# Attention weights transposed in 32 x 32 blocks on VectorE and moved by plain transfers; scores of eight heads at a time

## The chip, the cores and the metric

The kernel runs on one core of a Trainium2 chip. Time is device microseconds of one execution. Before the change three runs took 1278.85, 1280.2 and 1283.92 us; the median is 1280.2. A profile is a record of one execution by the hardware; in it PE is the matrix engine (TensorE), PEld its weight loads, DVE the vector engine (VectorE), ACT the scalar engine (ScalarE), POOL is GpSimd, and SP is SyncE, which here does nothing but issue DMAs.

## The reference

A cross-attention and a feed-forward block with simulated 8-bit quantization, each with a residual; the change touches the attention alone.

```python
# x [32, 100, 256], ctx [32, 361, 256], mask [1, 1, 100, 361]; 16 heads of 64
Q = einsum("btd,hdk->bhtk", layernorm(x), WQ)
K = einsum("btd,hdk->bhtk", ctx, WK)
V = einsum("btd,hdv->bhtv", ctx, WV)
attn = softmax(Q @ K^T / sqrt(64) + mask * -1e9)        # [b, h, 100, 361]
x = x + concat_heads(attn @ V) @ WO
x = x + ffn(layernorm(x))    # two linear layers of quantized inputs and weights, exact gelu between
```

Everything is float32 in the attention.

## The kernel before

There are 32 batches of 100 queries (`T`) and 361 keys (`S`), and 16 heads in 8 pairs (`NHP`); a pair's 128 features fill the 128 partitions. Two pairs, or four heads, make a quarter `q` (`PAIRS` = 2, `NQ` = 4). Keys are cut into `NSC` = 3 chunks of 128. Batches come in groups of `G` = 4; `j` is a batch's place in its group.

For each batch the matrix engine makes `kT` (keys, `k_part`, line 282), `v` (values, `v_part`, line 313), the scores `sc` (`products`, line 437: 100 queries by 361 keys a head; two heads of a pair occupy the upper and the lower 64 rows of the array side by side) and `av` (weights times values, `attend`, line 542). Once in a group it makes the queries of the next group (`pq`, `q_part`, line 374, in the last batch of a group) and projects the finished group (`py`, `project_T`, line 579, in the first). Per-batch outputs of that projection are transposed back (`project_back`, `po`) and added to x in `residual`.

Softmax: VectorE adds the mask and takes the row's extreme (`minima`, line 451) from PSUM into one of eight buffers of `pb`; ScalarE takes exponentials in place (`exponentials`, line 465); VectorE divides by the sum (`divide`, lines 473 and 480). The product with `v` needs the weights with keys on the partitions, so they must be transposed. In whole batches this takes four steps: GpSimd copies the float32 weights of a pair into `apart`, low and high 16-bit halves separated (`send`, line 505); SyncE issues one transposing DMA per pair into `xT` (line 514); ScalarE joins the halves into `pT` (`join`, line 521); `attend` of the next batch reads `pT`. The first and the last batch are done in parts instead, and their weights are transposed on the matrix engine (`weights_T`).

Thirty batches are whole. For them `whole_batch` writes out the order of each engine's instructions by hand: engines run in program order. In each of its four quarters stand the scores and minima of four heads, their exponentials, and the `k_part` of two pairs of the next batch. After the second quarter comes `attend` for the batch before; in the third and the fourth the three `v_part` of one half of the heads. `rest` ends the batch with layer-norm statistics, residuals and the group's work. PSUM tiles come from one pool of eight banks, taken in turn, so a new tile waits until the one eight places back has been read. DMAs issued on SyncE rotate over eight completion semaphores; one waits until the DMA eight places back has landed.

The 8-bit weights of the feed-forward block are prepared in pieces spread over the batches (`quantize_weight`); their overall maximum is found by GpSimd.

Of the kernel before, what the change touches and what calls it, by code (L numbers as in the profile page):

```python
# [27 lines left out]
def kernel(  # L28
# [15 lines left out]
    nc = tc.nc  # L44
# [19 lines left out]

    TH, RH = T // 2, P // 2
    TP = RH + TH
    TR = -(-T // 16) * 16
# [96 lines left out]
    with ExitStack() as att:  # L164
# [16 lines left out]
        maskt = wpool.tile([T, S], F32, tag="maskt", name="maskt")  # L181
# [5 lines left out]
        pb = wpool.tile([TP, NB, SP], F32, tag="p", name="p")  # L187
        for t in cbuf:
# [4 lines left out]
            wpool.tile([P, PAIRS, G, TP], F32, tag=f"q{q}", name=f"q{q}") for q in range(NQ)  # L193
# [5 lines left out]
        for q in range(NQ):  # L199
            clear(q, 0)  # L200

        apart = [
            wpool.tile([TR, 2 * NSC * 2 * SC], I16, tag=f"apart{k}", name=f"apart{k}")
            for k in range(2)
        ]
        for t in apart:
            nc.gpsimd.memset(t[T // 32 * 32 :], 0.0)

# [34 lines left out]
        nc.scalar.dma_start(out=maskt, in_=mask)  # L243
# [62 lines left out]
        def v_part(b, h, s):  # L306

            c = cbuf[b % NCB]
            if s == 0:
                vs[b, h] = p1.tile([SC, NSC, E // 2], F32, tag=f"v{h}", name=f"v{b}_{h}")  # L310
            pv = bank(f"pv{b}_{h}_{s}")
            for dc in range(NDC):
                nc.tensor.matmul(  # L313
                    pv[:SC, :],
                    c[:, dc, s * SC : (s + 1) * SC],
                    wvt[h][:, dc, :],
                    start=(dc == 0),
                    stop=(dc == NDC - 1),
                )
            return nc.vector.tensor_copy(vs[b, h][:, s, :], pv[:SC, :])  # L320
# [46 lines left out]
        def q_part(g, q):  # L367
# [3 lines left out]
            for pair in range(PAIRS):  # L371
# [12 lines left out]
                for j in range(G):  # L384
# [9 lines left out]
                    qbuf[q][:, pair, j0:j1, :T],  # L394
                    pq[:, j0 * T : j1 * T].rearrange("p (j t) -> p j t", t=T),
# [3 lines left out]
        pTs, aTs = {}, {}  # L399

        def weights_T(i, pair, on_vector):
# [5 lines left out]
            for h in range(2):  # L407
# [8 lines left out]
            pT = pTs[i, pair] = p1.tile(  # L416
                [SC, 2 * NSC, T], F32, tag=f"pT{pair}", name=f"pT{i}_{pair}"
            )
# [9 lines left out]
        def products(i, pairs):  # L428
# [3 lines left out]
            n = TP if halved(b) else T  # L432
# [13 lines left out]
        def minima(i, pss):  # L446

            for h, ps in pss.items():
                n = ps.shape[0]
                ms[h] = small.tile([TP, 1], F32, tag=f"m{h}", name=f"m{i}_{h}", bufs=1)  # L450
# [6 lines left out]
        def exponentials(i, heads):  # L457
            if i not in sums:
                sums[i] = [
                    small.tile([TP, 2 * NHP], F32, tag=t, name=f"{t}{i}") for t in ("rsum", "r")  # L460
                ]
            n = TP if halved(steps[i][0]) else T
# [6 lines left out]
        def divide(i, heads, at_once=4, after=None):  # L469
            rsum, r = sums[i]  # L470
            n = TP if halved(steps[i][0]) else T
# [25 lines left out]
        xTs, NX = {}, 3  # L497

        def send(i, q):

            n = NSC * 2 * SC
            for pair in range(q * PAIRS, (q + 1) * PAIRS):
                src = apart[pair % 2]
                for k in range(2):
                    nc.gpsimd.tensor_copy(  # L505
                        src[:T, k * n : (k + 1) * n].rearrange("t (c l s) -> t c l s", c=NSC, l=2),
                        pb[:T, (2 * pair + k) % NB, :].bitcast(I16).rearrange(
                            "t (c s l) -> t c l s", c=NSC, l=2
                        ),
                    )  # L510
                xT = xTs[i, pair] = p1.tile(
                    [SC, 2 * NSC * 2, TR], I16, tag="xT", name=f"xT{i}_{pair}", bufs=NX
                )
                nc.sync.dma_start_transpose(out=xT, in_=src)

        def join(i, q):
            for pair in range(q * PAIRS, (q + 1) * PAIRS):
                pT = pTs[i, pair] = p1.tile(
                    [SC, 2 * NSC, T], F32, tag=f"pT{pair}", name=f"pT{i}_{pair}"
                )  # L520
                nc.scalar.copy(  # L521
                    pT.bitcast(I16).rearrange("s c (t l) -> s c t l", l=2),
                    xTs[i, pair][:, :, :T].rearrange("s (c l) t -> s c t l", l=2),
                )

        def attend(i, pairs=None):
# [5 lines left out]
            g, j = b // G, b % G  # L532
            if first == 0 and j == 0:
                aTs[g] = p1.tile([P, NHP, G, T], F32, tag="aT", name=f"aT{g}")
            for p0 in range(first, first + n, HP):
                m = min(HP, n)
                av = bank(f"av{i}_{p0}")
                for pair in range(p0, p0 + m):
                    for c in range(NSC):
                        for k in range(2):  # L540
# [4 lines left out]
                                pTs[i, pair][:, k * NSC + c, :],  # L545
# [102 lines left out]
        def quantize_weight(src, rows, dst, name, n, after):  # L648

            cols = rows * dst.shape[2] // NWP  # L650
            if n == 0:
                w = wpool.tile([P, rows, dst.shape[2]], F32, tag="wst", name=f"w{name}")
                load = nc.gpsimd.dma_start(out=w, in_=src.rearrange("(c p) f -> p c f", p=P))
                tc.add_manual_dep(load.ins, after.ins.name, SYNC)
                am = small.tile([P, NWP], F32, tag="am", name=f"am{name}")
                scales[name] = w.rearrange("p c f -> p (c f)"), am
                return
            wf, am = scales[name][:2]
            if n <= NWP:
                i = nc.vector.tensor_reduce(  # L660
                    am[:, n - 1 : n], wf[:, (n - 1) * cols : n * cols], AX.X, ALU.max,
                    apply_absolute_value=True,
                )
                tc.add_manual_dep(i.ins, after.ins.name, ORDER)
            if n == NWP:
                al = small.tile([P, NWP], F32, tag="aal", name=f"aal{name}")
                nc.gpsimd.partition_all_reduce(al, am, P, bass_isa.ReduceOp.max)
                scales[name] = wf, al
            if n == NWP + 1:
                sw = const.tile([P, 1], F32, tag=f"sw{name}", name=f"sw{name}")  # L670
                rw = small.tile([P, 1], F32, tag="rw", name=f"rw{name}")
                nc.vector.tensor_reduce(sw, am, AX.X, ALU.max)
                nc.vector.tensor_scalar(sw, sw, 1.0 / 127.0, 1e-8, ALU.mult, ALU.max)
                nc.vector.reciprocal(rw, sw)
                scales[name] = wf, sw, rw
            if n > NWP:
                p = slice((n - NWP - 1) * cols, (n - NWP) * cols)
                wi = small.tile([P, cols], I16, tag="wi", name=f"wi{name}_{n}")
                nc.scalar.activation(wi, wf[:, p], AF.Copy, bias=0.0, scale=scales[name][2])
                return lambda: nc.vector.tensor_scalar(  # L680
                    dst.rearrange("p c f -> p (c f)")[:, p], wi, 127.0, -127.0, ALU.min, ALU.max
                )

# [9 lines left out]
        nc.vector.tensor_scalar(maskt, maskt, 1e9, None, ALU.mult)  # L693
        warm(bank("warm0"), 7)
        k_start()
        for h in range(2):
# [4 lines left out]
        q_part(0, 0)  # L701

        todo = [
            n if n is None else (w, n)
            for w in ("1", "2") for n in (0, None, *range(1, 2 * NWP + 1))
        ]
        weights = {"1": (w1T, NDC, w1qt), "2": (w2T, NFC, w2qt)}

        def rest(i, ended, last, after=None):
# [3 lines left out]
            for h in ended:  # L715
# [3 lines left out]
                if k == 2 * (G - 2) + 1 and not whole(i):  # L719
                    ln1(g + 1, after)  # L720
                if g >= 1 and 2 <= k < 2 + G:
                    project_back(g - 1, k - 2)
                if k == 2 * (G - 2) + 1:
                    ln1_T(g + 1)
# [3 lines left out]
                if g >= 1 and k == 1:  # L728
# [3 lines left out]
        def part_of_batch(i):  # L732
# [6 lines left out]
            first_copied = None  # L739
            last = scores(i)  # L740
            if i >= 1:
                if whole(i - 1):
                    join(i - 1, NQ - 1)
                attend(i - 1)
            if b >= 1:
                for h in begun:
                    for c in range(NSC):
                        done = v_part(b, h, c)
                        if h == begun[0] and c == 0:
                            first_copied = done  # L750
# [7 lines left out]
            rest(i, ended, last, first_copied)  # L758
# [6 lines left out]
        def whole_batch(i):  # L765
# [5 lines left out]
            late = []  # L771
# [3 lines left out]
            for q in range(NQ):  # L775
                heads = range(2 * PAIRS * q, 2 * PAIRS * (q + 1))
                minima(i, products(i, range(q * PAIRS, (q + 1) * PAIRS)))
                if q == 1:
                    divide(i, range(2 * PAIRS))
                    send(i, 0)  # L780
                exponentials(i, heads)
                if q == 0 and b - 1 + NCB < B:
                    load_ctx(b - 1 + NCB)
                n = steps[i + 1][2] // NQ
                for pair in range(q * n, (q + 1) * n):
                    k_part(i + 1, pair)
                if q == 0 and whole(i - 1):
                    join(i - 1, NQ - 1)
                if q == 1:
                    attend(i - 1)  # L790
                    last = divide(i, heads)
                    send(i, 1)
                    for piece in todo[:2]:
                        if piece is not None:
                            w, p = piece
                            late.append(quantize_weight(*weights[w], w, p, last))
                    del todo[:2]
                if q >= 2:
                    join(i, q - 2)
                    for c in range(NSC):  # L800
                        v_part(b, q - 2, c)
                        if c == 0:
                            divide(i, heads)
                            send(i, q)
                if q == 2:
# [384 lines left out]
```

## Time and profile before

| what | value |
|---|---|
| median of three runs | 1280.2 us |
| the profiled execution's own time | 1282.56 us |
| its span in the profile | 1280.8 us |
| granted TensorE clock, mean | 0.993 |
| instructions | 21412 |
| packets moved by DMA | 355220, of which under 512 B 332094 |
| hardware queue of SyncE, share of the 16 DMA engines | 44.3% |
| DMA issues on SyncE for the weights | 240 (`xT<-apart`), 8 a batch |

How to read it: a page of the profile gives each engine's busy time and share of the span, the chain of work that ended last (followed back from the last instruction, at each step to what released it), and groups of instructions by source line with their count, busy time, mean duration, and the idle time before them with what ended it. The trace behind it also answers with a timeline of an engine (start, duration, what) and with a table of busy times by window. Instructions on one engine overlap at their ends, so the distance from start to start is what one costs in a row of them. A busy share of a matrix engine says that it always had an instruction in flight, not that each ran at its best.

### The profile page before, as it was taken

The numbers are of one execution on the slowest core, as the hardware profiler recorded it, in microseconds if no ns is written. First come the engines' busy times: TensorE is split into PE (matmuls) and PEld (weight loads), VectorE is DVE, ScalarE is ACT, GpSimd is POOL, SyncE is SP. The second block draws the span as 40 slices with busy tenths as digits, with TensorE's granted clock in tenths as the row PEclk, the third lists the DMA queues.
The fourth block names the chain that finished last, engine by engine and source line by source line (L and its number), as shares of the span: only waits on it lengthen the run. The fifth ranks groups of instructions, "written<-read, shape, count | busy, mean of one in ns | idle before, by whom it ended". The sixth has DMA issues, their size and how long they took to land.

```text
span 1280.8 us, 21412 instructions
## 1 busy us (share of the span) xinstructions
PE 1249.6 (98%) x7184; PEld 703.2 (55%) x7184; DVE 863.8 (67%) x2409; ACT 817.8 (64%) x1720; POOL 510.3 (40%) x674
## 2 busy tenths in 40 slices
PE   9999999989999999999999999999999999999858
PEld 4655555555555555555555555555555555556426
DVE  4577574776557765786657764787647774686897
ACT  2567566665476855674666755676657754764876
POOL 2044333462435532553435532554335533462250
PEclk9999999999999999999999999999999999999989
DMA  8165534474445543555445543555345534551113
GB/s 241 50 131 99 99 62 81 79 142 77 88 66 96 114 79 66 103 105 99 78 75 105 97 74 77 102 102 105 59 76 104 105 67 85 87 97 25 60 46 104
DMA packets 355220, 115.50 MB, mean 90 GB/s; under 512 B 332094, under 2 KB 353158, under 8 KB 355110
## 3 DMA queue, kind: packets, MB, share of 16 engines
q1 hardware_dynamic: 352032, 107.42, 44.3%
q0 software_dynamic: 2144, 5.38, 1.3%
q10 hardware_dynamic: 934, 1.34, 0.3%
q8 instruction: 56, 0.92, 0.3%
q14 instruction: 54, 0.44, 0.1%
HBM read 24.97 MB, written 6.55 MB: 25 GB/s over the span
## 4 chain that ended last, share of the span: by engine, by line
PE 89%; DVE 4%; ACT 3%; issue 2%; DMA 1%; POOL 1%; SPq 0%; DVEq 0%; ACTq 0%; POOLq 0%
PE pk L282 24%; PE pv L313 24%; PE sc L437 13%; PE av L542 11%; PE pq L374 7%; PE py L579 6%; ACT h L1032 2%; PE pf L1136 2%; DVE p L480 1%; DVE v L320 1%; PE po L563 1%; PE warm L161 1%; DMA wvt<-in_wv_dram 1%; ACT xqT L942 0%; PE pt L411 0%
## 5 line engine op out<-in xcount | busy, mean ns | idle before, releaser
L505 POOL COPY apart<-p 100x768 int16<-100x768 int16 x480 | 396.8, 860 | 609.0 <-DVE p L480 411.8
L465 ACT ACTIVATE p<-p,m 100x361 f32<-100x361 f32 (+1 forms) x512 | 299.1, 588 | 252.6 <-DVE m L451 252.0
L282 PE MATMUL pk<-c,wkt 128*128 128x361 f32 x1016 | 341.5, 479 | 0.3 <-ACT xnT L365 0.3
L313 PE MATMUL pv<-wvt,c 128*128 128x512 f32 x768 | 340.2, 592 | 1.0 <-DMA wvt<-in_wv_dram 1.0
L521 ACT COPY pT<-xT 128x1200 int16<-128x1200 int16 x240 | 309.8, 1336 | 34.9 <-DMA xT<-apart 34.9
L451 DVE CUSTOM_DVE_ANT_0 p<-sc,maskt 100x361 f32<-100x361 f32 x480 | 227.2, 529 | 131.1 <-PE sc L437 120.9
L480 DVE TENSOR_SCALAR p<-p,r 100x361 f32<-100x361 f32 (+1 forms) x512 | 266.5, 583 | 4.4
L282 PEld LDWEIGHTS pk<-c,wkt 128*128 128x128 f32 x1016 | 183.0, 189 | 152.4 <-issue 44.5
L313 PEld LDWEIGHTS pv<-wvt,c 128*128 128x128 f32 x768 | 145.7, 190 | 168.9 <-issue 147.3
L320 DVE COPY v<-pv 128x512 f32<-128x512 f32 x192 | 127.2, 682 | 137.7 <-PE pv L313 137.5
L437 PE MATMUL sc<-kT,q 64*100 64x361 f32 (+1 forms) x1024 | 191.4, 484 | 0.4
L542 PEld LDWEIGHTS av<-pT,v 128*64 128x64 f32 x3072 | 134.3, 138 | 22.0 <-issue 6.1
L542 PE MATMUL av<-pT,v 128*64 128x100 f32 x3072 | 141.5, 252 | 3.7 <-ACT kT L289 3.7
L437 PEld LDWEIGHTS sc<-kT,q 64*100 64x100 f32 (+1 forms) x1024 | 78.3, 163 | 91.9 <-issue 16.3
L289 ACT COPY kT<-pk 128x361 f32<-128x361 f32 x254 | 102.1, 448 | 27.9 <-PE pk L282 27.9
L465 ACT ACTIVATION_READ_ACCUMULATOR p<-p,m 100x1 f32 (+1 forms) x512 | 96.8, 189 | 0.0
L374 PE MATMUL pq<-xnT,wqt 128*128 128x400 f32 x256 | 87.9, 500 | 0.2 <-ACT xnT L365 0.2
L579 PE MATMUL py<-aT,wot 128*128 128x400 f32 x224 | 76.4, 499 | 0.0
L374 PEld LDWEIGHTS pq<-xnT,wqt 128*128 128x128 f32 x256 | 48.4, 190 | 38.8 <-issue 3.3
L579 PEld LDWEIGHTS py<-aT,wot 128*128 128x128 f32 x224 | 42.6, 190 | 34.0 <-issue 3.3
L586 ACT COPY yT<-py 128x400 f32<-128x400 f32 x14 | 6.9, 492 | 84.9 <-PE py L579 84.9
L473 DVE RECIPROCAL r<-rsum 100x4 f32<-100x4 f32 (+2 forms) x131 | 22.5, 172 | 56.4 <-ACT p L465 56.1
(142 smaller groups left out, 722.3 us busy)
## 6 DMA issues: line engine op xcount, KB each, us to landing
c<-in_ctxT_dram SPq DMA_DIRECT2D x31, 361.0 KB
xT<-apart SPq DMA_TRANSPOSE x240
x<-in_x_dram SPq DMA_DIRECT2D x8, 400.0 KB
xb<-xb POOLq DMA_DIRECT2D x32, 100.0 KB, 2.2
x<-xb SPq DMA_DIRECT2D x5, 384.0 KB
out_dram<-x SPq DMA_DIRECT2D x5, 256.0 KB
out_dram<-x SPq DMA_DIRECT2D x3, 384.0 KB
wqt<-in_wq_dram SPq DMA_DIRECT2D x4, 256.0 KB
```

The source lines that it names most:

```text
L282: nc.tensor.matmul(pk[:, :S], wkt[q][:, dc, col * P : (col + 1) * P], c[:, dc, :S], start=(dc == 0), stop=(dc == NDC - 1),)
L313: nc.tensor.matmul(pv[:SC, :], c[:, dc, s * SC : (s + 1) * SC], wvt[h][:, dc, :], start=(dc == 0), stop=(dc == NDC - 1),)
L320: return nc.vector.tensor_copy(vs[b, h][:, s, :], pv[:SC, :])
L374: nc.tensor.matmul(pq[:, :GT], wqt[q][:, dc, pair * P : (pair + 1) * P], xnTs[g][:, dc, :], start=(dc == 0), stop=(dc == NDC - 1),)
L437: nc.tensor.matmul(pss[h], qbuf[pair // PAIRS][k * DK : (k + 1) * DK, pair % PAIRS, b % G, :n], kT[k * DK : (k + 1) * DK, pair, :], start= ...
L451: done = nc.vector.tensor_tensor_reduce(pb[:n, h % NB, :S], ps, maskh if halved(steps[i][0]) else maskt, 1.0, BIG, ALU.add, ALU.min, ms[h] ...
L465: nc.scalar.activation(s, s, AF.Exp, bias=ms[h][:n], scale=-1.0, accum_out=sums[i][0][:n, h : h + 1])
L480: nc.vector.tensor_scalar(s, s, r[:n, h : h + 1], None, ALU.mult)
L505: nc.gpsimd.tensor_copy(src[:T, k * n : (k + 1) * n].rearrange("t (c l s) -> t c l s", c=NSC, l=2), pb[:T, (2 * pair + k) % NB, :].bitcast ...
L521: nc.scalar.copy(pT.bitcast(I16).rearrange("s c (t l) -> s c t l", l=2), xTs[i, pair][:, :, :T].rearrange("s (c l) t -> s c t l", l=2),)
L542: nc.tensor.matmul(av[k * DK : (k + 1) * DK, (pair - p0) * T : (pair - p0 + 1) * T], vs[b, pair // HP][:, c, h * DK : (h + 1) * DK], pTs[i ...
L579: nc.tensor.matmul(py[:, :GT], wot[:, c, dc * P : (dc + 1) * P], aT[:, c, :, :].rearrange("p j t -> p (j t)"), start=(c == 0), stop=(c == ...
```

## The change

1. **Transposition.** The copies into `apart`, the transposing DMAs and `join` are gone. Queries now lie in four blocks of 25 on partitions 0 to 24, 32 to 56, 64 to 88 and 96 to 120 (`QB` = 32, `NQB` = 4, `TB` = 25): `q_part` writes them so, with zeros between, the mask is loaded so, and scores have 128 stationary columns instead of 100. `blocks` transposes, on VectorE, one head's 128 x 384 weights within each block of 32 x 32, into an `xT` tile that holds four heads; there are two such tiles. `send` then carries the block of queries `k` and key block `m` from partitions 32k to 32m with a plain DMA on SyncE: 16 DMAs for four heads, each of 32 partitions x 3 chunks x 100 floats, 38.4 KB.
2. **pT** becomes two tiles of eight heads (`wide`), with a query block's 25 columns of a head in four runs, 200 floats apart; `attend` reads them in that form as the moving operand.
3. **Order.** `whole_batch` works in two halves of eight heads: eight scores, the minima, six exponentials, two `k_part`, two exponentials, two `k_part`, and then division, transposition and sending of two quarters. `attend` stands in the first half. The six `v_part` come after both halves in one run, those of the second half of the heads copied by ScalarE instead of VectorE. `rest` is split into `residuals` and `group_work`.
4. **Weights' maxima.** `weight_pieces` finds the overall maximum with two small transposes on the matrix engine and reductions on VectorE instead of GpSimd's reduction over partitions.

```diff
-        maskt = wpool.tile([T, S], F32, tag="maskt", name="maskt")
+        maskt = wpool.tile([P, S], F32, tag="maskt", name="maskt")
+        nc.gpsimd.memset(maskt, 0.0)
...
-        nc.scalar.dma_start(out=maskt, in_=mask)
+        for k in range(NQB):
+            nc.scalar.dma_start(
+                out=maskt[k * QB : k * QB + TB], in_=mask[k * TB : (k + 1) * TB]
+            )
...
-            return nc.vector.tensor_copy(vs[b, h][:, s, :], pv[:SC, :])
+            copy = nc.scalar.copy if h and not halved(b) else nc.vector.tensor_copy
+            return copy(vs[b, h][:, s, :], pv[:SC, :])
...
                 nc.vector.tensor_scalar(
-                    qbuf[q][:, pair, j0:j1, :T],
-                    pq[:, j0 * T : j1 * T].rearrange("p (j t) -> p j t", t=T),
+                    qbuf[q][:, pair, j0:j1, :].rearrange("p j (k t) -> p j k t", t=QB)[..., :TB],
+                    pq[:, j0 * T : j1 * T].rearrange("p (j k t) -> p j k t", k=NQB, t=TB),
                     -1.0 / DK**0.5, None, ALU.mult,
                 )
...
-        xTs, NX = {}, 3
+        xTs, NX, NH = {}, 2, 2 * PAIRS
+
+        def blocks(i, heads):
+            q = heads[0] // NH
+            xTs[i, q] = p1.tile(
+                [P, SP // QB, NH * TB + QB - TB], F32, tag="xT", name=f"xT{i}_{q}", bufs=NX
+            )
+            for h in heads:
+                nc.vector.transpose(
+                    xTs[i, q][:, :, h % NH * TB : h % NH * TB + QB],
+                    pb[:, h % NB, :].rearrange("t (c s) -> t c s", s=QB),
+                )
 
         def send(i, q):
-            n = NSC * 2 * SC
-            for pair in range(q * PAIRS, (q + 1) * PAIRS):
...
-                    nc.gpsimd.tensor_copy(
...
-                nc.sync.dma_start_transpose(out=xT, in_=src)
-
-        def join(i, q):
...
-                nc.scalar.copy(
...
+            src = xTs[i, q].rearrange("p (c m) t -> p c m t", c=NSC)
+            half, t0 = divmod(q * NH * TB, NHP * TB)
+            dst = wide(i, half).rearrange("s (c k) t -> s c k t", c=NSC)[..., t0 : t0 + NH * TB]
+            for m in range(P // QB):
+                for k in range(NQB):
+                    nc.sync.dma_start(
+                        out=dst[m * QB : (m + 1) * QB, :, k, :],
+                        in_=src[k * QB : (k + 1) * QB, :, m, : NH * TB],
+                    )
...
+            def weights(pair, k, c):
+                if not whole(i):
+                    return pTs[i, pair][:, k * NSC + c, :]
+                h = 2 * (pair % HP) + k
+                return wide(i, pair // HP)[:, c * NQB : (c + 1) * NQB, h * TB : (h + 1) * TB]
...
-                                pTs[i, pair][:, k * NSC + c, :],
+                                weights(pair, k, c),
...
-            for q in range(NQ):
-                heads = range(2 * PAIRS * q, 2 * PAIRS * (q + 1))
-                minima(i, products(i, range(q * PAIRS, (q + 1) * PAIRS)))
...
+            if b - 1 + NCB < B:
+                load_ctx(b - 1 + NCB)
+            for half in range(2):
+                heads = range(half * NHP, (half + 1) * NHP)
+                minima(i, products(i, range(half * HP, (half + 1) * HP)))
+                n = steps[i + 1][2] // 2
+                keys = range(half * n, (half + 1) * n)
+                exponentials(i, heads[:6])
+                for pair in keys[: n // 2]:
+                    k_part(i + 1, pair)
+                exponentials(i, heads[6:])
+                for pair in keys[n // 2 :]:
+                    k_part(i + 1, pair)
+                for q in range(half * NQ // 2, (half + 1) * NQ // 2):
+                    divide(i, range(2 * PAIRS * q, 2 * PAIRS * (q + 1)))
+                    blocks(i, range(2 * PAIRS * q, 2 * PAIRS * (q + 1)))
+                    send(i, q)
+                if half == 0:
+                    attend(i - 1)
+            residuals(i, range(2), None)
+            if j == G - 2:
+                ln1_T(g + 1)
+            v_part(b, 0, 0)
...
+            for c in range(1, NSC):
+                v_part(b, 0, c)
+            while later:
+                normalize(later.pop(), None)
+            for c in range(NSC):
+                v_part(b, 1, c)
+            if j == G - 3:
+                ln1(g + 1)
+            group_work(i, range(2))
```

## The prediction

> **What bounds the kernel now.** I read the busy shares and the chain of waits first.
>
> ```profile
> PE 1249.6 (98%) x7184; PEld 703.2 (55%) x7184; DVE 863.8 (67%) x2409; ACT 817.8 (64%) x1720; POOL 510.3 (40%) x674
> PE 89%; DVE 4%; ACT 3%; issue 2%; DMA 1%; POOL 1%; SPq 0%; DVEq 0%; ACTq 0%; POOLq 0%
> ```
>
> TensorE is busy 98% and is 89% of the chain. Shares average over stages, so the table by window comes next, from one `av` stage to the next: two plain batches, and two that also hold `py` or `pq`.
>
> ```profile
> 687.75:719.51 31.76, 31.76 (x198) 18.07 (x200) 25.80 (x74) 22.96 (x52) 15.59 (x21) 1.00 0.57 100
> 719.51:760.89 41.38, 41.38 (x218) 22.91 (x220) 25.80 (x71) 26.72 (x56) 15.99 (x21) 1.00 0.45 84
> 655.91:687.75 31.84, 31.78 (x191) 17.48 (x192) 23.50 (x73) 22.07 (x50) 18.41 (x26) 1.00 0.58 102
> ```
>
> TensorE fills every batch: 31.8 us in a plain one, 41.4 in a long one. So the POOL copies, the DMA transposes and the `join` copies, long as they are, stand beside TensorE; removing them buys nothing by itself. A gain must come out of TensorE's own rows:
>
> ```profile
> 611.83 2.69 PE L282 MATMUL pk<-c,wkt 128*128 128x361 f32 x8
> 614.46 4.34 PE L542 MATMUL av<-pT,v 128*64 128x100 f32 x96
> 618.73 1.46 PE L437 MATMUL sc<-kT,q 64*100 64x361 f32 x8
> 620.12 2.69 PE L282 MATMUL pk<-c,wkt 128*128 128x361 f32 x8
> 622.65 5.31 PE L313 MATMUL pv<-wvt,c 128*128 128x512 f32 x12
> 627.89 1.46 PE L437 MATMUL sc<-kT,q 64*100 64x361 f32 x8
> ```
>
> From start to start, `pk` takes 2.63 us before `av` and 2.53 before `pv`: a change of stationary shape costs time. Single starts show a score group of four heads as 0.384, 0.303, 0.308 and 0.397 us per pair of heads, of which 0.30 is streaming; the `pk` behind it begins with 0.408 instead of 0.303.
>
> **TensorE's part of the change.** Eight heads together: 0.384 + 6 x 0.305 + 0.397 = 2.61 us against 2 x 1.39, so 0.35 saved a batch. `pk` in runs of 16: 5.05 against 5.25 and 4.96 against 5.06, 0.30 saved. `pv` in one run: 0.09. Stationary 128 columns instead of 100: loads run inside the 0.30 us slots, except one per group, whose exposed part was 0.083 us at 100 columns (first start to load-bound second) and 0.106 at 128 (`pk`): 2 x 0.024 back. Net **0.7 us a batch**. The four one-row transposes for the weights' scale are under 1 us in all.
>
> `av` now streams 100 columns as four runs of 25, 800 B apart. No row has a strided moving operand. Below nothing is excluded, since the columns are the same. The nearest row is `av` itself (43.6 ns an instruction); at an assumed tenth more it would cost 0.43 us a batch, 13 in all. The Trainium skill (SBUF — State Buffer, Door 1: The DMA port swizzle) says that a 16-byte line read at least twice in a row goes at full rate; runs of 25 floats meet that but for at most one line each. I take nothing.
>
> **What leaves.** Per batch 16 POOL copies, 8 transposing DMAs and 8 `join` copies:
>
> ```profile
> L505 POOL COPY apart<-p 100x768 int16<-100x768 int16 x480 | 396.8, 860 | 609.0 <-DVE p L480 411.8
> L521 ACT COPY pT<-xT 128x1200 int16<-128x1200 int16 x240 | 309.8, 1336 | 34.9 <-DMA xT<-apart 34.9
> ```
>
> VectorE's divisions then run undisturbed; four took either of these:
>
> ```profile
> 654.85 2.49 DVE L480 TENSOR_SCALAR p<-p,r 100x361 f32<-100x361 f32 x4
> 658.95 1.36 DVE L480 TENSOR_SCALAR p<-p,r 100x361 f32<-100x361 f32 x4
> ```
>
> Start to start 0.32 us each when POOL is quiet, about 0.9 beside a POOL copy.
>
> **What VectorE gets.** 16 transposes of 384 columns. Not in the trace; the nearest row, the minima (361 columns), repeats every 0.455 us, which scales to **0.48**; bounds 0.4 and double, 0.9. A plain batch: 16 x 0.455 minima, 16 x 0.32 divisions, 0.8 reciprocals, 16 x 0.48 transposes, 1.8 for three `v` copies (the other three go to ScalarE, which loses 310 us), two residuals with statistics 3.5, normalizing 0.7, some 1.6 for semaphore waits ahead of the transposes (an estimate from the 21 ns records): 28.5 of 31.1 us. It fits, without much room. ScalarE isn't late: with 0.58 us an exponential, heads 0 to 3 are ready 2.9 us after the first minimum, when VectorE is still at its eight minima (3.7), and heads 6 and 7, behind two `kT` copies of 0.35, after 6.0, before the first division and its transposes end (7.1). Eight score tiles fill all eight PSUM banks, so the `pk` behind them waits for the first minimum, done 1.5 us after the scores begin and needed at 2.61: free, unless VectorE comes late to it.
>
> **What only moves.** The context load stands at the head of the batch, ahead of the first send on SyncE, 0.5 us counted below. The residuals, `ln1_T` and `ln1` change places within the batch with the same instructions; VectorE does the residuals before the `v` copies, counted below. The weights' maxima leave POOL (two reductions of 0.4 us) for VectorE and TensorE; their 1 MB loads stay on POOL. Three more mask loads of some 0.45 us stand on ScalarE's queue before its first copy at 10.1 us; the first scores come after 23 us, so that is hidden; without that cover it would cost 1.4 us once.
>
> **What SyncE gets: the step that decides.** 4 sends of 16 transfers, 64 a batch instead of 8, each 32 partitions x 3 x 400 B = 38.4 KB. The packets are light: 256 B packets took 18 ns and 1024 B ones 46, so 400 B is about 23, six per engine, 0.15 us. The queue's own timeline shows what an issue costs:
>
> ```profile
> 12.85 0.37 SPq L222 DMA_DIRECT2D wqt<-in_wq_dram  x1
> 13.27 0.47 SPq L222 DMA_DIRECT2D wkt<-in_wk_dram  x1
> 13.78 0.47 SPq L222 DMA_DIRECT2D wqt<-in_wq_dram  x1
> 14.29 0.98 SPq L215 DMA_DIRECT2D c<-in_ctxT_dram  x2
> 15.32 0.47 SPq L250 DMA_DIRECT2D wot<-in_wo_dram  x1
> 15.83 14.69 SPq L228 DMA_DIRECT2D x<-in_x_dram  x7
> ```
>
> Back to back, each with one satisfied wait, as in `send`, the pitch is **0.512 us** (13.27, 13.78, 14.29, 15.32 after two, 15.83). Without a wait, at the start, it was 0.46; alone, 0.37 plus a 0.045 gap, 0.42. I take 0.51, the row nearest in kind. The Trainium skill (DMA: Bandwidth & Descriptors, Issuing engines are not separate DMA queues) calls the sequencer's issue time usually small relative to the DMA itself. By it SyncE hides and the sum is TensorE's alone, 30 x 0.7 = 21 us gained. By the row 64 x 0.512 + 0.3 for the extra waits + 0.5 for the context load = **33.6 us a batch**, above the 31.1 that TensorE wants in a plain one. The row decides.
>
> What queues behind it: let A be the start of `av` for the previous batch. The first send waits until that `av` has read the first half of `pT`, A + 2.45. There are two `xT` tiles, so the transposes of the fourth quarter wait for the second send: A + 2.45 + 32 x 0.512 + 0.15 + 1.0 for landing (the last output DMA began at 1277.67 us, took 0.35 to issue, and its last packet ended at 1279.23, 1.2 later with eight 1 KB rows per engine; here there are six short ones) = A + 20. Behind them on VectorE: 2.3 of transposes and waits, residuals 3.5, `v` 1.8, normalizing 0.7, the next batch's first minimum 0.55, which frees the bank of the next `pk`, then 5.05 of `pk`: the next `av` at A + 33.9. So both the queue and this chain give 33.6 to 33.9; a plain batch grows from 31.8 to **33.7**. Long batches, 41.4, swallow it and lose 0.7.
>
> **Sum.** The chain has about 15 plain and 15 long intervals: 15 x 1.9 = +28; 15 x 0.7 = -10.5. At 270 us the present kernel once waits 4.78 us for `xT` with a slower `av` after it (5.79 instead of 4.27), 6 us in all; half of that may vanish, -3. Together +14.5: the profiled execution's 1282.6 (span 1280.8 and 1.8 around it) becomes 1297; it lay 2.4 above the median 1280.2, so I forecast **1295**.
>
> **Rivals.**
> 1. *SyncE keeps up, faster.* Decided by the pitch alone. At 0.46 the VectorE chain is A + 32.2: 15 x 0.4 - 13.5 gives 1273; at 0.42 nothing waits: -24, 1256. For it: the pitches without a wait, and that TensorE does lose work. Against: each transfer carries a wait. It is faster below 0.46 and slower above 0.49. Chance 0.24.
> 2. *The two cancel,* pitch 0.46 to 0.49, 1274 to 1286. Chance 0.14.
> 3. *VectorE becomes the bound:* transposes at 0.9 us add 6.4 to 28.5, and waits on `xT` on top: 35.4 a plain batch, 15 x 3.6 - 13.5, 1321. Nothing in the trace speaks for half rate, but nothing shows the operation. Chance 0.14.
> 4. *TensorE cools:* idle gaps of 2 us each may cost clock; after the 3.7 us gap at 270 the granted clock was 0.90 in that stretch. 15 x 1.5 on top of the forecast, 1317. Chance 0.08.
>
> The forecast itself has 0.40, with its own range 1284 to 1308. What a measurement can tell from no change is 0.5%, 6.4 us: faster below 1273.8, slower above 1286.6. From the cases: faster 0.24, same 0.14, slower 0.62. The range goes from 1256 (pitch 0.42) to 1330 (case 3 with some of case 4).
>
> **What would show it.** TensorE: score groups 2.6 us, `pk` runs 5.0, `av` still 4.27 when not waiting; long intervals 40.7. SyncE: 16 issues of a send in 8.2 us and no rest in plain batches. VectorE: a gap before the fourth quarter's transposes, released by a DMA; divisions 0.32 apart; transposes 0.48. Plain intervals near 33.7. I am wrong if SyncE idles in plain batches (issue under 0.46), if plain intervals fall to 31, or if transposes need 0.9.

## The result, and the profile after

The changed kernel takes **1508.1 us** (median of 4 runs, 1506.6 to 1509.6) against 1280.7 before (4 runs, 1278.9 to 1283.9): ratio 1.177, 95% interval 1.1745 to 1.180. The forecast was 1295, slower, with a range up to 1330. The sign and the place were right; the size was not.

The page of the changed kernel, its span, its busy shares and its chain of waits:

```profile
span 1505.7 us, 22604 instructions
PE 1349.9 (90%) x7186; PEld 774.8 (51%) x7188; DVE 959.9 (64%) x2803; ACT 584.9 (39%) x1570; POOL 111.9 (7%) x195
SPq 39%; PE 36%; DVE 7%; issue 6%; DMA 5%; POOL 5%; ACT 1%; DVEq 0%; ACTq 0%; POOLq 0%
```

Before, TensorE was 89% of the chain and SyncE's queue 0%. Now the largest share, 39%, is SyncE's issuing. The timeline of SyncE in the middle of the program (start us, duration us, what, count):

```profile
898.15 43.23 SPq L533 DMA_DIRECT2D pT<-xT  x64
941.48 0.53 SPq L215 DMA_DIRECT2D c<-in_ctxT_dram  x1
942.12 42.55 SPq L533 DMA_DIRECT2D pT<-xT  x64
984.78 0.53 SPq L215 DMA_DIRECT2D c<-in_ctxT_dram  x1
```

Sixty-four issues took 43.23 us, 0.675 each, and the next batch began 0.64 us after the context load did. There is no rest: 43.97 us from one batch to the next, where the forecast had 33.6. Nor does SyncE stand for its eight semaphores: a transfer lands 1.9 us after its issue begins (median), and eight issues take over 5 us. The same batches on TensorE, and its waits:

```profile
887.72 5.12 PE L285 MATMUL pk<-c,wkt 128*128 128x361 f32 x16
892.77 3.31 PE L561 MATMUL av<-pT,v 128*64 128x100 f32 x72
898.81 1.26 PE L561 MATMUL av<-pT,v 128*64 128x100 f32 x24 [2.73 <-DMA pT<-xT]
900.00 2.70 PE L451 MATMUL sc<-kT,q 64*128 64x361 f32 x16
902.63 5.12 PE L285 MATMUL pk<-c,wkt 128*128 128x361 f32 x16
907.59 10.46 PE L316 MATMUL pv<-wvt,c 128*128 128x512 f32 x24
```

The last quarter of `av`, 24 instructions, stands 2.73 us for its transfers. VectorE waits at the other end of the same queue; these are the lines with the largest such waits (total us, times, longest):

```profile
DVE xT L521 <- DMA pT<-xT: 369.4, 81, 7.8
PE av L561 <- DMA pT<-xT: 53.0, 21, 7.5
```

From the third start of `av` (67.6 us before, 66.9 now) to that of the last whole batch (1153.8 and 1370.2) there are 30 intervals, 14 of them long, with `py` or `pq` in them, and 16 plain. They summed to 1086.2 us before and to **1303.3** now, 43.4 each, which is SyncE's time for a batch. Long and plain ones no longer differ: they have means of 43.6 and 43.3 us now, and had 41.5 and 31.6 before. The sum grew by 217.1; the stretch after them is 8.6 longer and the one before 0.7 shorter, in all the 225 us by which the span grew. TensorE, which now rests, shows a granted clock of 0.921 over the span against 0.993.

### The profile page after: what moved, and what is told of

Same layout as the page of the kernel before. It is cut to its first block, busy times and chain, and to the rows that moved or that the text cites. A ratio compares the mean times of both kernels' runs of the same rounds, so it can differ in the third digit from the quotient of the medians.

```text
span 1505.7 us, 22604 instructions
## 1 busy us (share of the span) xinstructions
PE 1349.9 (90%) x7186; PEld 774.8 (51%) x7188; DVE 959.9 (64%) x2803; ACT 584.9 (39%) x1570; POOL 111.9 (7%) x195
## 4 chain that ended last, share of the span: by engine, by line
SPq 39%; PE 36%; DVE 7%; issue 6%; DMA 5%; POOL 5%; ACT 1%; DVEq 0%; ACTq 0%; POOLq 0%
SPq L533 39%; PE pk L285 9%; PE pv L316 9%; PE pq L378 5%; DMA pT<-xT 4%; PE sc L451 4%; PE py L598 4%; PE av L561 3%; DVE xT L521 2%; PE pf L1164 1%; POOL xb L143 1%; DVE p L465 1%; POOL rstd L646 1%; ACT h L1060 1%; DVE x L150 1%
## 5 line engine op out<-in xcount | busy, mean ns | idle before, releaser
L521 DVE STREAM_TRANSPOSE xT<-p 128x384 f32<-128x384 f32 x480 | 277.7, 579 | 399.0 <-DMA pT<-xT 369.4
L479 ACT ACTIVATE p<-p,m 128x361 f32<-128x361 f32 (+1 forms) x512 | 299.1, 587 | 304.8 <-DVE m L465 304.8
L451 PE MATMUL sc<-kT,q 64*128 64x361 f32 (+1 forms) x1024 | 253.4, 557 | 54.1 <-DVE rmax L622 46.2
L465 DVE CUSTOM_DVE_ANT_0 p<-sc,maskt 128x361 f32<-128x361 f32 x480 | 222.9, 529 | 42.7 <-PE sc L451 42.4
L451 PEld LDWEIGHTS sc<-kT,q 64*128 64x128 f32 (+1 forms) x1024 | 121.4, 214 | 165.6 <-DVE rmax L622 64.8
L494 DVE TENSOR_SCALAR p<-p,r 128x361 f32<-128x361 f32 (+1 forms) x512 | 174.3, 404 | 4.4
L324 ACT COPY v<-pv 128x512 f32<-128x512 f32 x90 | 52.8, 586 | 256.4 <-PE pv L316 256.4
L568 ACT COPY aT<-av 128x400 f32<-128x400 f32 (+2 forms) x67 | 31.9, 476 | 175.8 <-PE av L561 175.8
L479 ACT ACTIVATION_READ_ACCUMULATOR p<-p,m 128x1 f32 (+1 forms) x512 | 96.1, 188 | 0.0
L324 DVE COPY v<-pv 128x512 f32<-128x512 f32 x102 | 65.0, 676 | 12.5 <-PE pv L316 12.4
```

Source lines behind the costliest of these rows:

```text
L324: return copy(vs[b, h][:, s, :], pv[:SC, :])
L451: nc.tensor.matmul(pss[h], qbuf[pair // PAIRS][k * DK : (k + 1) * DK, pair % PAIRS, b % G, :n], kT[k * DK : (k + 1) * DK, pair, :], start= ...
L465: done = nc.vector.tensor_tensor_reduce(pb[:n, h % NB, :S], ps, maskh if halved(steps[i][0]) else maskt, 1.0, BIG, ALU.add, ALU.min, ms[h] ...
L479: nc.scalar.activation(s, s, AF.Exp, bias=ms[h][:n], scale=-1.0, accum_out=sums[i][0][:n, h : h + 1])
L494: nc.vector.tensor_scalar(s, s, r[:n, h : h + 1], None, ALU.mult)
L521: nc.vector.transpose(xTs[i, q][:, :, h % NH * TB : h % NH * TB + QB], pb[:, h % NB, :].rearrange("t (c s) -> t c s", s=QB),)
```

## The experiments

The question was why an issue costs 0.66 and not 0.51, and whether that is all. The rivals: the number of issues (**Theory 1**), the two `xT` tiles, which tie VectorE to the queue (**Theory 2**), and the bytes and packets behind the issues (**Theory 3**). Each kernel ran once where no number of runs is given. The pitch is the time from the start of one issue to the start of the next.

**The issue by itself (issue).** A bench in which nothing of the layer is computed: sixteen DMAs of one form after another from SyncE, for six forms between SBUF and SBUF (four are shown), one of them again from ScalarE, four weight loads and the output stores.

```diff
+    for n in range(N):      # da: the form of the change
+        nc.sync.dma_start(out=da[:32, n], in_=s4[32:64, :, 1, :100])
+    for n in range(N):      # db: 32 x 100
+        nc.sync.dma_start(out=db[32:64, n], in_=s4[:32, 0, 1, :100])
+    for n in range(N):      # dc: 32 x 3 x 200
+        nc.sync.dma_start(out=dc[64:96, n], in_=s4[32:64, :, 1, :200])
+    for n in range(N):      # dd: 128 x 3 x 100
+        nc.sync.dma_start(out=dd[:, n], in_=s4[:, :, 1, 100:200])
```

> Nothing of the attention or the feed-forward block is computed; the kernel only issues DMAs back to back on SyncE, 16 of each form, and writes zeros as output. In the changed kernel one issue of 32 partitions x 3 x 100 floats took 0.597 us and the next began 0.642 after it. If the pattern's dimensions set the cost: form a (32 x 3 x 100) 0.64 us again, c (32 x 3 x 200) and d (128 x 3 x 100) the same, b (32 x 100) and e (128 x 100) about 0.46 to 0.51, f (32 x 2 x 100) like a. If the number of rows sets it: d, with four times the rows of a, well over 0.7, and b well below e. If the bytes set it: c longer than a. If it is peculiar to the large kernel: a about 0.51 here.

SyncE's timeline of the bench:

```profile
4.01 12.73 SPq L65 DMA_DIRECT2D da<-src  x16
16.79 10.09 SPq L68 DMA_DIRECT2D db<-src  x16
26.92 10.27 SPq L71 DMA_DIRECT2D dc<-src  x16
37.23 10.79 SPq L74 DMA_DIRECT2D dd<-src  x16
```

Divide the last three by 16: 0.63 to 0.67 us an issue. The first form, that of the change, has a median pitch of 0.655; one gap of 2.7 us makes its row longer. ScalarE issued the same form at the same time, every 0.657 us: two queues side by side hardly slowed each other. Against the 0.641 that the form of the change has alone (next run), a third of the bytes (`db`), twice the bytes (`dc`) and four times the rows (`dd`) cost the same within 5%, so that neither dimensions nor rows nor bytes set the pitch, and it isn't peculiar to the large kernel. The two weight loads from DRAM that follow each other in this bench were 0.517 apart, near the row that the forecast had used. So the row was read rightly, but it wasn't a row of this operation.

**Which ends (ends).** The form of the change with its ends in SBUF or DRAM, and on fewer partitions; nothing of the layer is computed.

```diff
+    for n in range(N):      # sa: SBUF to SBUF
+        nc.sync.dma_start(out=sa[:32, n], in_=here)
+    for n in range(N):      # db: SBUF to DRAM
+        nc.sync.dma_start(out=rb[:32, n], in_=here)
+    for n in range(N):      # sc: DRAM to SBUF
+        nc.sync.dma_start(out=sc[:32, n], in_=away)
+    for n in range(N):      # de: DRAM to DRAM
+        nc.sync.dma_start(out=re[:32, n], in_=away)
```

> Nothing of the layer is computed: only DMA issues from SyncE, 16 of each kind, back to back. The form of the change (32 partitions x 3 x 400 B) with its ends in SBUF or DRAM. Theory A (an issue costs by its ends: two in SBUF are the dearest): SBUF to SBUF 0.64 us again, SBUF to DRAM near 0.41, DRAM to SBUF near 0.51, at the same 38.4 KB. Theory B (an issue costs by its form, 32 rows of three 400 B pieces): all four kinds at about 0.64. The same form SBUF to SBUF on 16, 8 and 4 partitions: if the cost goes with the engines or rows that take part, it falls below 0.6 with 8 or 4; if it is the instruction's own, it stays at 0.64.

```profile
4.47 10.26 SPq L73 DMA_DIRECT2D sa<-src  x16
14.77 7.67 SPq L76 DMA_DIRECT2D db<-src  x16
22.48 7.38 SPq L79 DMA_DIRECT2D sc<-away  x16
29.91 10.04 SPq L82 DMA_DIRECT2D de<-away  x16
50.82 11.69 SPq L87 DMA_DIRECT2D sh<-src  x16
```

The same 38.4 KB cost 0.641 us from SBUF to SBUF, 0.472 to DRAM, 0.464 from DRAM, and 0.633 from DRAM to DRAM (medians). Theory B falls. Theory A had the direction of the two mixed kinds (forecast 0.41 and 0.51), but the last kind shows that what is dear is not SBUF at both ends but **both ends in the same memory**. The packets don't explain it: they were of 400 B where the source was in SBUF and of 1200 B where it was in DRAM, and with either source it was the destination in the other memory that was cheaper. Why, these runs don't show. On 8 partitions (`sh`) it was 0.729, on 4 it was 0.690: fewer rows don't make it cheaper.

**A third of the data (third).** All 64 transfers, each with one chunk of its three; the other two chunks of the weights are zeros.

```diff
-                        out=dst[m * QB : (m + 1) * QB, :, k, :],
-                        in_=src[k * QB : (k + 1) * QB, :, m, : NH * TB],
+                        out=dst[m * QB : (m + 1) * QB, 0, k, :],
+                        in_=src[k * QB : (k + 1) * QB, 0, m, : NH * TB],
```

> The changed kernel with only the first of three key chunks carried by each of the 64 transfers of a batch (32 partitions x 100, two dimensions); the other chunks of pT are set to zero by GpSimd, so attention sees a third of the weights. Theory 1, SyncE's issue is the limit: the time follows the pitch of this form; at 0.50 us 64 x 0.50 + 0.9 = 33 us a plain batch, some 1290 us; at 0.64 no change from 1508. Theory 3, the transfers' bytes or packets are the limit: a third of them, so well below 1300 even if the pitch stays at 0.64.

```profile
888.64 41.94 SPq L534 DMA_DIRECT2D pT<-xT  x64
```

1490.7 us, pitch 0.633 (median). Two thirds of the transfers' packets gone bought 17 us of 227: bytes and packets are not the limit, and Theory 3 falls.

**Four tiles (nx4).** `NX` = 4 instead of 2; to make room, the feed-forward weights' preparation is left out.

```diff
-        xTs, NX, NH = {}, 2, 2 * PAIRS
+        xTs, NX, NH = {}, 4, 2 * PAIRS
```

> The changed kernel with four xT tiles instead of two; to make room, the preparation of the 8-bit feed-forward weights is left out (they are constants). Theory 1, SyncE's issue is the limit: 64 issues of 0.66 us stay, VectorE's 369 us of waiting shrink or move, and the time stays at 1490 to 1508. Theory 2, VectorE's wait for one of two xT tiles holds up the minima and so the scores: the time falls to 1250 to 1320.

```profile
PE av L561 <- DMA pT<-xT: 172.9, 32, 9.3
```

1499.4 us: VectorE's 369 us of waiting for the queue are gone, `av` waits 173 us for its transfers instead of 53, and the time stays. Theory 2 falls as the cause of the loss.

**Half the issues (eight, then eightfull).** Eight heads in a tile, so that a transfer is 32 partitions x 3 x 800 B and a batch needs 32. In `eight` the feed-forward weights' preparation is left out; in `eightfull` it is there, with the weights loaded in 1 KB pieces, twice, so that the wider tiles fit.

```diff
-        xTs, NX, NH = {}, 2, 2 * PAIRS
+        xTs, NX, NH = {}, 2, NHP
...
-                    send(i, q)
+                send(i, half)
```

> The changed kernel with eight heads in an xT tile and one send per half: 32 transfers a batch of 32 partitions x 3 x 200, the same bytes; the preparation of the 8-bit feed-forward weights is left out. Theory 1: SyncE needs 32 x 0.66 + 0.8 = 22 us a batch and hides, TensorE is the limit again: plain intervals 31.1, long 40.7, 1245 to 1262 us. Theory 3, bytes: no change, about 1500. Theory 2 would also allow about 1255, since each tile then has half a batch more time; nx4 tells it apart.

> The changed kernel with eight heads in a tile instead of four: 32 transfers of 32 partitions x 3 x 800 B a batch, and the feed-forward weights loaded twice in 1 KB pieces so that the wider tiles fit. Theory 1 (SyncE's issues are the whole loss): 32 x 0.655 + 0.8 = 21.8 us a batch hides beside TensorE; plain intervals 31.1, long ones 40.7, 1258 to 1268 us, faster than before by 1 to 1.7%. Rival (the lighter weights' preparation of the earlier eight-head kernel was part of its 1262): 1275 or more.

1262.0 us for `eight` (one run), and for `eightfull` **1260.0** (4 runs, 1259.4 to 1262.3) against 1280.8: ratio 0.983, interval 0.981 to 0.985. The rival of `eightfull` falls with it: the weights' preparation costs nothing that shows here. SyncE and TensorE in `eightfull`:

```profile
891.19 22.17 SPq L534 DMA_DIRECT2D pT<-xT  x32
913.46 0.53 SPq L215 DMA_DIRECT2D c<-in_ctxT_dram  x1
931.88 22.30 SPq L534 DMA_DIRECT2D pT<-xT  x32
```

```profile
908.76 10.91 PE L599 MATMUL py<-aT,wot 128*128 128x400 f32 x32
919.60 2.71 PE L451 MATMUL sc<-kT,q 64*128 64x361 f32 x16
922.23 5.12 PE L285 MATMUL pk<-c,wkt 128*128 128x361 f32 x16
927.28 4.35 PE L562 MATMUL av<-pT,v 128*64 128x100 f32 x96
931.56 2.70 PE L451 MATMUL sc<-kT,q 64*128 64x361 f32 x16
```

Thirty-two issues take 22.2 us; in this long batch SyncE then rests 18 us, and TensorE goes from stage to stage without a wait. Plain intervals are 31.1 to 31.4 us, but for three shorter ones at the ends, long ones 40.7 to 41.0.

The Trainium skill (Perfetto Trace Analysis, What "DMA-bound" means) names this kind of bound: the issuing engine's track solid with DMA slices. It has large descriptors (the pieces into which a DMA is cut) as the remedy. The trace agrees with the first. To the second it adds that the size of the pieces does nothing by itself: those of 800 B (`dc`) were issued no faster than those of 400 B (`sa`), 0.641 against 0.641. What helped was half as many transfers, each twice as large.

**Another queue (poolhalf).** The other way out, every second transfer from GpSimd's queue:

```diff
-                    nc.sync.dma_start(
+                    (nc.gpsimd if m % 2 else nc.sync).dma_start(
```

> The changed kernel with every second transfer issued by GpSimd's queue: 32 a batch on SyncE, 32 on GpSimd. Theory 1 (the loss is the issuing queue, not the 64 transfers): SyncE 32 x 0.655 + 0.8 = 21.8 us a batch, GpSimd, nearly idle otherwise, at up to 0.9 us each 29 us; both under 31.1, so 1256 to 1275 us. Rival (64 transfers a batch are too many for whatever moves them, or GpSimd's issue costs 1 us and more): 32 us and more a batch, 1290 us and above.

1334.5 us, the rival's side, but not by either of its reasons: GpSimd's issue had a median pitch of only 0.537 us, and SyncE rests again. GpSimd's timeline in a plain batch:

```profile
885.90 4.95 POOL L533 DMA_DIRECT2D pT<-xT  x9 [2.05 <-PE ptx L366]
891.12 3.78 POOL L533 DMA_DIRECT2D pT<-xT  x7 [0.27 <-DMA pT<-xT]
894.92 0.26 POOL L645 TENSOR_SCALAR v<-mv 100x1 f32<-100x1 f32 x1
```

The residual's step at 894.92 had its input when VectorE's statistics of the first residual ended, at 890.90, and stood behind 7 issues. VectorE's normalizing then waits for GpSimd:

```profile
899.14 0.73 DVE L150 TENSOR_SCALAR x<-x,mv,rstd 100x256 f32<-100x256 f32 x2 [4.83 <-POOL xb L143]
```

Behind it `pk` stood 1.67 us for VectorE's first minimum. Over the whole program (total us, times, longest):

```profile
DVE x L150 <- POOL xb L143: 61.4, 13, 7.1
PE pk L285 <- DVE m L465: 54.1, 15, 8.6
```

The first was 14.0 us in the changed kernel. The second was 6.2 us in `eightfull`, and those 48 us more are most of the 74.5 us between the two remedies. Moving an issue delays what is queued behind it on the other engine.

**Is the pitch all? (fifty, fifty4).** With 50 of the 64 transfers SyncE's batch costs some 34 us, about what the forecast had thought for 64. The blocks left out of the weights are zeros, written by GpSimd. `fifty4` adds four `xT` tiles, with the weights in 1 KB pieces as in `eightfull`.

```diff
+                nc.gpsimd.memset(wides[b, half][96:, :, :], 0.0)
...
+                    if m == 3 and k >= 1 - q % 2:
+                        continue
```

> The changed kernel with 50 of the 64 transfers of a batch; the blocks left out are zeros, so that part of the weights is missing from the sums. If only the pitch of the forecast's sum was wrong, 50 x 0.655 + 0.3 + 0.5 = 33.6 us of SyncE a batch, which is what the forecast had for 64, and its other terms then hold: plain intervals near 33.7, long ones near 40.7, some 1295 us (1285 to 1305). If something else of the change costs as well (two tiles, the slower transposes, a cooler TensorE), plain intervals stay above 36 and the time above 1320.

> The kernel with 50 transfers a batch (blocks left out are zeros), now with four xT tiles instead of two and the feed-forward weights loaded in 1 KB pieces to make room. In the run with two tiles SyncE needed 34 us a batch, but plain intervals took 37 to 39: VectorE's fourth transposes waited 4 us for a tile, and the residuals, GpSimd's steps, the normalizing and the next minimum queued behind them. Theory V (that chain behind the xT tiles holds the plain batch once SyncE is lighter): with four tiles the transposes don't wait, plain intervals fall to 34 to 35 (SyncE's 33.2 plus the landing), long ones stay 40.7, some 1300 to 1330 us. Rival (SyncE's load itself, or TensorE cooled by idling, holds it): plain intervals stay at 36.5 or more, 1370 or more.

1397.7 and 1347.3 us. In both the first `av` comes late, at 54.4 and 55.4 us against 31.7. The clearing changed GpSimd's order at the start: the first group's `rstd` stands behind it and behind a broadcast, at 36.0 us in `fifty` instead of 15.5. That is an artefact of the experiment, and without it they would be near 1375 and 1324, an estimate. The 30 intervals are free of it: 1178.4 (39.3 each) and 1121.9 (37.4), where the forecast's 33.7 and 40.7 have a mean of 37.2.

So in `fifty` 12 of the 14 long intervals are at 40.7 or 40.8, as forecast, but the plain ones have a mean of 37.3, in the middle in pairs of 39 to 41 and 35 to 38. The first of such a pair, from its `av` at 881.83 (A), VectorE, then TensorE:

```profile
902.45 2.42 DVE L522 STREAM_TRANSPOSE xT<-p 128x384 f32<-128x384 f32 x4 [4.23 <-DMA pT<-xT]
...
908.46 1.88 DVE L324 COPY v<-pv 128x512 f32<-128x512 f32 x3
912.08 0.73 DVE L150 TENSOR_SCALAR x<-x,mv,rstd 100x256 f32<-100x256 f32 x2 [1.75 <-POOL xb L143]
912.73 1.38 DVE L350 TENSOR_SCALAR xn<-x,mv,rstd 100x256 f32<-100x256 f32 x4
914.03 0.53 DVE L466 CUSTOM_DVE_ANT_0 p<-sc,maskt 128x361 f32<-128x361 f32 x1
```

```profile
914.62 6.66 PE L285 MATMUL pk<-c,wkt 128*128 128x361 f32 x16 [3.16 <-DVE m L466]
```

The fourth transposes start at A + 20.6 (A + 20 in the forecast). Then the forecast's chain lacks 1.75 us for GpSimd's step of the residual, which VectorE's normalizing needs, and 1.3 us for the next group's `xn`, which only the first of each pair holds. And `pk`, after 3.16 us of idle, takes 6.6 us instead of 5.05: its row in the table by window has a granted clock of 0.76 (column after the busy times), the next `pk` 1.00. The trace's record of the clock has half speed from 910.93 to 917.76 us and full speed on either side.

```profile
914.62:921.21 6.59, 6.59 (x17) 3.74 (x17) 6.45 (x23) 5.87 (x19) 0.00 (x0) 0.76 0.36 92
928.11:933.07 4.96, 4.96 (x18) 3.08 (x17) 3.45 (x15) 4.76 (x17) 0.00 (x0) 1.00 0.27 59
```

The sum is A + 39.4 instead of A + 33.9. With four tiles that chain is cut: plain intervals come in pairs of 31.4 and 33.5 to 37.4 and have a mean of 33.2, a little under Theory V's 34 to 35. The long ones with `pq` rise to 41 to 47, where `av` waits for the queue's backlog. As measured, 1347 lies outside Theory V's 1300 to 1330; less the artefact, 1324 lies inside.

**The transposes (vtr).** Nothing of the layer is computed; 16 transposes in each of three layouts of the output.

```diff
+    for n in range(N):      # over: 25 columns apart, overlapping by 7
+        nc.vector.transpose(over[:, :, n % 4 * 25 : n % 4 * 25 + 32], pc)
+    for n in range(N):      # apart: 32 columns apart
+        nc.vector.transpose(apart[:, :, n % 4 * 32 : n % 4 * 32 + 32], pc)
```

> Nothing of the layer is computed: 16 transposes of 128 x 384 on VectorE in each of three layouts of the output, nothing else running. Theory A (the pitch of 0.613 in the changed kernel comes from each output overlapping the one before by 7 columns, so that each waits for the end of the last): 0.61 again with the blocks 25 columns apart, 0.46 to 0.50 with 32 columns apart and with one contiguous output. Theory B (the operation itself is that slow): 0.61 in all three.

VectorE's timeline of the bench, and the group in the changed kernel:

```profile
11.73 4.67 DVE L62 STREAM_TRANSPOSE apart<-p 128x384 f32<-128x384 f32 x10
16.32 7.43 DVE L65 STREAM_TRANSPOSE whole<-p 128x384 f32<-128x384 f32 x16
```

```profile
L521 DVE STREAM_TRANSPOSE xT<-p 128x384 f32<-128x384 f32 x480 | 277.7, 579 | 399.0 <-DMA pT<-xT 369.4
```

The pitch was 0.46 us, so Theory B falls: the operation isn't slow. But Theory A isn't shown either. The overlapping ones had 0.46 too, for in the bench the first two layouts came out interleaved, and none of them began after the end of the one just before it. In the changed kernel the transposes of a group do: each waits on a semaphore that the one before it raises, the trace has 34 to 35 ns of idle between them, and 0.579 + 0.034 is the 0.613 from start to start. That the overlap is the reason for that wait fits, but no run shows it.

## Why the prediction was right or wrong

**The step that failed** is the term "64 x 0.512 + 0.3 for the extra waits + 0.5 for the context load = 33.6 us a batch". The pitch came from loads that have one end in DRAM ("I take 0.51, the row nearest in kind"); the transfers of the change go from SBUF to SBUF. The trace of before had no plain transfer of that kind, but it had a warning. Its only issues from SBUF to SBUF, the transposing DMAs, took far longer than the weight loads' 0.4 to 0.5 us (ns, shortest, median, longest):

```profile
L514 SPq DMA_TRANSPOSE xT<-apart x240: 1259/1363/2734, 68.8 to 1152.1; - x120
```

Alone the transfers of the change cost 0.64, and in the kernel 0.66 to 0.68: a median of 0.641, and 57 of the 1920 issues longer than 0.7 us, 1.26 on average. A batch is 64 x 0.641 = 41.0 us, 0.64 for the context load, some 1.3 for the long issues and a rest of half a microsecond. No rival allowed for a pitch above 0.512: the forecast looked for errors below it alone, and the top of its range, 1330, came from other engines.

Where the long issues come from can be read in the trace's packets. The instructions themselves are loaded by DMA too, and one of the queues brings them in pieces of 16 KB (packets, MB, share):

```profile
q8 instruction: 58, 0.95, 0.3%
```

While the weights were sent, 49 of these 58 pieces moved. Of the 57 long issues 47 had one under way and ended 0.39 us after it (median), and only 2 of the 49 pieces lengthened no issue. Why an issue stands for such a piece isn't shown.

The mechanism, a plain batch bound by SyncE's issues, was right. So was it to set the row above the remark in the Trainium skill (DMA: Bandwidth & Descriptors, Issuing engines are not separate DMA queues) that issue time is usually small relative to the DMA itself: six packets an engine, some 0.15 us by the forecast's estimate, stand against 0.64 for the issue, and even the landing comes only 1.3 us after the issue's end. Put into the sum, 43.4 us of SyncE a batch exceeds the 40.7 of long batches as well, so that "Long batches, 41.4, swallow it" fails with the same term: 30 intervals of 43.4 instead of 15 of 33.7 and 15 of 40.7.

**A second error was hidden behind it.** The VectorE chain, "the next `av` at A + 33.9", lacked GpSimd's step, `xn` and the cooled `pk`. Had the pitch been such that SyncE needed 33.6, the time would have been near 1375 by `fifty`, an estimate, not 1295. The rival of a cooling TensorE, taken apart from the forecast at 1.5 us a plain batch, is part of it: 1.54 us in the `pk` shown, and 13 of the 59 full runs of `pk` in `fifty` took 7.1 us on average.

**Right, by the runs:**
- TensorE's pieces, start to start in `eightfull`: `sc` 2.63 (2.61 forecast), `pk` 5.05 and 4.96 (as forecast), `av` 4.28 with its strided operand, 4.27 before (nothing taken), intervals 31.1 to 31.4 and 40.7 (31.1 and 40.7). That the gain was 20.8 us where the forecast has 21 for a SyncE that hides is partly luck: it holds the one wait of 6 us near 270 us, now gone, and an end that is 3.8 us longer.
- VectorE's gap before transposes, released by a DMA: 369 us in all, in 81 waits where one a batch was forecast.
- Divisions 0.32 apart: 0.317, with the POOL copies gone (mean duration 404 ns against 583).

**Wrong, without effect here:** transposes 0.613 apart instead of 0.48, 2.1 us of VectorE a batch, inside the bounds; `eightfull` hides them. The forecast's third rival has a slip, 6.4 us for what 0.9 us a transpose would add (16 x 0.42 is 6.7); nothing hangs on it.

**The rivals.** "SyncE keeps up" ends where `eightfull` is; the sum that it needs, less than 31 us of SyncE a batch, was reached by halving the count, at an unchanged pitch. VectorE didn't become the bound: it is busy 64%, and waits.

## What to carry to other kernels

A DMA occupies its queue for a time that, for the small transfers here, depended on the two memories and hardly on what it carried. Count the issues per stage and multiply by a pitch measured between the same two memories, before asking about bytes; where no row of that kind exists, let the range reach above the nearest row as well as below it. When a stage is fed by many small transfers, try fewer and larger ones before moving them to another queue; where they do move, look at what is queued behind them there. And where a forecast adds one long chain of waits, list every engine that a step of it waits for, and allow for a slower first run of TensorE after a gap.

## What the runs showed of the hardware

- Issue pitch for 38.4 KB on SyncE: SBUF to SBUF 0.641 us, DRAM to DRAM 0.633, mixed 0.464 and 0.472; SBUF to SBUF from 12.8 KB to 153.6 KB and from 32 to 128 rows 0.63 to 0.67. GpSimd issued the same transfer every 0.537 us, ScalarE every 0.657 beside a busy SyncE.
- An issue that ran beside a 16 KB load of instructions ended 0.39 us after it: 47 issues of the changed kernel, 1.37 us long on average instead of 0.6.
- TensorE after 3.2 us of idle: 6.6 us for a run of 5.0, granted clock 0.76; over the changed kernel 0.921. Not every gap did this: four runs of `pk` in `poolhalf` came after gaps of 1.3 to 2.6 us and had the full clock.
- VectorE transposes 128 x 384 floats within blocks of 32 every 0.46 us, 0.613 where each waits for the one before.
